# A four-layer graph attention kernel on one core: one pool for the forms of the rows and of elu, an 18th weight buffer, one copy of G further ahead, and other due groups

## The chip, the core and the metric

The kernel runs on one core of one Trainium2 chip. The metric is the device time of one execution in microseconds (us); the time of the kernel before is the median of three runs. Engines are named as the profile names them: PE (TensorE's matmuls), PEld (its loads of stationary operands), DVE (VectorE), ACT (ScalarE), POOL (GpSimd) and SP (SyncE, which issues nearly all DMAs here).

## What is computed

Sixteen graphs of 1024 nodes with 256 features share one adjacency matrix and pass through four graph attention layers, each behind a normalisation and with a residual. Layers 0 and 2 have four heads of 64, layers 1 and 3 one head of 256. The reference, cut to layers 1 and 3 (in layers 0 and 2 the same is done for each head):

```python
# for l in 0..3
h = jnp.maximum(_layernorm(x, axis=-1), 0.0)
x = x + gat_l(h, adj, W_l, a_l)

# layer 1
Wh = jnp.matmul(h, W)
e_src = jnp.matmul(Wh, a[:D]); e_dst = jnp.matmul(Wh, a[D:])
e = e_src + jnp.swapaxes(e_dst, 1, 2)
e = jnp.where(e > 0, e, ALPHA * e)          # leaky ReLU, 0.2 (0.01 in layer 3)
e = jnp.where((adj > 0)[None], e, -jnp.inf)
h_prime = jnp.matmul(jax.nn.softmax(e, axis=-1), Wh)
return jax.nn.elu(h_prime)                  # relu in layer 3
```

## The kernel before

*Tiles and steps.* A graph is held as 8 blocks of 128 nodes. The work is 64 steps, each one layer of one graph; four graphs are in flight, and `order_of_steps` interleaves them so that from step 7 on a four-head step (odd numbers, to 59) and a one-head step (even numbers) alternate. A pair of steps takes 74.6 us. n is the number of a step below.

*A step on TensorE.* The exponential of a leaky ReLU is written as a product of factors of row and column and a maximum: W[j, i] = max(G[i], r[j]) * mask[j, i]. `broadcast` (L383) copies the row G of a head, spread over 128 partitions, from an SBUF buffer gs into PSUM; `weights` (L388) makes a tile W of 128 x 1024 on VectorE, eight per head; `aggregate` (L404) multiplies W with the projected rows `whx` and adds up in PSUM, and ScalarE takes the result out (L419). A step has eight groups k of such matmuls: in a four-head step a head and half of its nodes, in a one-head step one block. Some 3.5 to 3.7 us of matmuls make a group. PSUM has four `bank` buffers for the results and two for G.

*Preparing a step.* `preparation(n)` returns 21 pieces in a fixed order: statistics of each half of the rows (L240, VectorE), their combination (POOL), normalisation of each half (L285, ACT), then for each half its transposition and four projections (L327 on PE, taken out by ACT at L329), and then `factors`, `rows`, the fetch of G's rows and a mark. A half is transposed by DMA: `split` (L294, ACT) separates the two 16-bit halves of each value, a DMA on SP (L296) transposes them, and `merge` (L302, ACT) puts them together. `rows` transposes the factors on TensorE (L351), copies them (gT, L353) and writes them to DRAM by a DMA on SP (`grow`, L355); `fetch` reads one head's G back, spread over all partitions, by another (`gs`, L371, 512 KB). The piece for the last use of gs is the copy of G (L383) on ACT.

*What sets the order.* Every engine runs its instructions in the order in which they are written, and so does SP, which holds back a DMA until what it needs has arrived, with all behind it. The order comes from a plan. Each kind of step has a tuple of 21 due groups, counted from 8 (n - 2), the start of the step two before: FOUR and SHORT (L50, L51) for four-head steps, ONE and TIGHT for one-head steps, SOON, FIRST and LATE for the beginning and special cases. Index 11 is the split of the second half, index 12 its merge, 7 to 10 and 13 to 16 the projections. In the main loop (L608 to L628), each group does in turn: what is left of its own W tiles, its matmuls (`aggregate`), parts of finishing the step before (`ending`), copies of G ahead (`emit_heads`), a piece of setting up a layer (`later`), the pieces of preparation that are due (`prepare`), and W tiles ahead (`emit_tiles`), up to 6 or 3 beyond those made, and no more than WBUFS beyond those used up. `fetch_heads` issues the fetches of gs up to two heads ahead of the copies of G.

*Finishing a step.* `finish` divides by the sum, applies elu and adds to x. elu has a buffer `e` of 128 x 1024 for each half (L447); its parts are due at groups 0 to 3 of the next step, results of layer 3 are stored at group 4.

*Buffers.* The pool `prep` has two buffers `e` and five `rows` (HBUFS), used for all forms of the rows (normalised, split, transposed, merged); `work` has 17 buffers for W (WBUFS). Each of them is 4 KB per partition. A pool hands out the buffer that was released longest ago, and the first instruction on it waits for its last reader.

*Setting up a layer.* `weight_columns(l)` makes columns of the weights from the attention vectors in four pieces: `vectors` (a DMA into a buffer `e`, L141), `spread` (a matmul and a copy on ACT, L149 and L152), `columns` (VectorE, L159 and on) and `bound`. For layers 1 to 3 they are done in the main loop, at groups 0, 1, 2 and 8 from 1, 27 and 43 (L605 to L607).

Of the kernel before, what the change touches and what calls it, by code (L numbers as in the profile page):

```python
# [26 lines left out]
F32 = mybir.dt.float32  # L27
# [9 lines left out]
P = 128  # L37
EPS = 1e-5
SHIFT = 60.0
STREAMS = 4  # L40
WBUFS = 17
HBUFS = 5

# [1 line left out]

FOUR = (-8, -8, -5, 0, 2, 1, 4, 5, 5, 5, 5, 3, 4.5, 5, 5, 5, 5, 6, 8, 8, 10)  # L50
SHORT = (-4, -4, -4, 0, 2, 1, 4, 5, 5, 5, 5, 3, 4.5, 5, 5, 5, 5, 6, 8, 8, 10)  # L51
ONE = (2, 2, 2, 3, 4, 3, 5, 7, 7, 7, 7, 4, 7, 8, 8, 8, 8, 8, 11, 11, 12)
SOON = (0, 0, 0, 1, 2, 1, 3, 4, 4, 5, 5, 2, 5, 6, 6, 7, 7, 7, 8, 8, 10)
FIRST = (-4, -4, -4, -2, -0.9, -1, -1, -0.8, -0.8, -0.8, -0.8, 0, 0, 1, 1, 1, 1, 1, 2, 2, 4)
# [13 lines left out]
def kernel(ctx: ExitStack, tc: tile.TileContext, x, adj, ws, avs, out):  # L68
# [64 lines left out]
    def weight_columns(l):  # L133

        H, slope, hs, _ = LAYERS[l]
        D = F // H
        st = {}

        def vectors(queue=nc.sync):

            st["a"] = prep.tile([P, HALF, H, D], F32, name="e")  # L141
            queue.dma_start(
                out=st["a"][0:1, 2:4],
                in_=bass.AP(tensor=avs[l].tensor, offset=avs[l].offset,
                            ap=[[0, 1], [D, 2], [hs, H], [1, D]]))

        def spread():
            pa = bank(2, H, D)
            nc.tensor.matmul(pa.rearrange("p t h d -> p (t h d)"), lhsT=ones[0:1, :],  # L149
                             rhs=st["a"][0:1, 2:4].rearrange("p t h d -> p (t h d)"),  # L150
                             start=True, stop=True)
            nc.scalar.activation(st["a"][:, 0:2], pa, AF.Copy)  # L152

        def columns(ks=range(K)):
            for k in ks:
                for part in range(2):
                    prod = st["a"][:, 2 + part]
                    wk = heads_of(wx[l], H)[:, k]
                    nc.vector.tensor_mul(prod, wk[:, :, 0:D], st["a"][:, part])  # L159
                    nc.vector.tensor_reduce(  # L160
                        wk[:, :, D] if part else wx[l][:, k, F + H:F + 2 * H], prod, AX.X, ALU.add)
            if K - 1 not in ks:
                return
            st["sq"] = small.tile([P, K, H], F32, name="sq", bufs=1)
            wd = heads_of(wx[l], H)[:, :, :, D]
            nc.vector.tensor_tensor(st["sq"], wd, wd, op=ALU.mult)

        def bound():

            pn = bank(H)  # L170
            for k in range(K):
                nc.tensor.matmul(pn, lhsT=ones, rhs=st["sq"][:, k, :], start=(k == 0),
                                 stop=(k == K - 1))
            top = small.tile([P, 1], F32, name="top", bufs=1)
            nc.vector.tensor_reduce(top, pn, AX.X, ALU.max)
            nc.gpsimd.tensor_tensor(top, top, half1, op=ALU.pow)
            nc.gpsimd.tensor_scalar(cbias[l], top, 16.01, None, op0=ALU.mult)
            nc.gpsimd.tensor_scalar(nbias[l], top, -16.01 * slope, None, op0=ALU.mult)
            nc.gpsimd.tensor_scalar(rbias[l], top, -16.01 * (1.0 - slope), SHIFT,
                                    op0=ALU.mult, op1=ALU.add)  # L180

        return vectors, spread, columns, bound
# [242 lines left out]
    def finish(n):  # L425

        b, l = steps[n]
        H = LAYERS[l][0]
        D = F // H
        st = state[n]  # L430

        def views(half):
            s = slice(half * HALF, (half + 1) * HALF)
            return (xs[b][:, s, :].rearrange("p c (h d) -> p (c h) d", h=H),
                    st["y"][:, s, :, 0:D].rearrange("p c h d -> p (c h) d"),
                    st["r"][:, s, :].rearrange("p c h -> p (c h)"))

        def divide():
            st["r"] = small.tile([P, C, H], F32, name="r")
            nc.vector.reciprocal(st["r"], st["y"][:, :, :, D])  # L440

        def scaled(half):
            xh, yh, r = views(half)
            rb = r[:, :, None].to_broadcast([P, HALF * H, D])
            if l < L - 1:

                e = st["e", half] = prep.tile([P, HALF * H, D], F32, name="e")  # L447
                if H > 1 and slack(n):
                    nc.vector.scalar_tensor_tensor(e, yh, 0.0, rb, op0=ALU.min, op1=ALU.mult)  # L449
            nc.gpsimd.tensor_tensor(yh, yh, rb, op=ALU.mult)  # L450
            if l < L - 1 and not (H > 1 and slack(n)):
                nc.gpsimd.tensor_scalar(e, yh, 0.0, -3.0e38, op0=ALU.min, op1=ALU.max)  # L452

        def exponential(half):
            if l < L - 1:
                nc.scalar.activation(st["e", half], st["e", half], AF.Exp)  # L456

        def add(half):
            xh, yh, r = views(half)
            if l < L - 1:  # L460
                e = st["e", half]
                nc.vector.scalar_tensor_tensor(e, e, -1.0, yh, op0=ALU.add, op1=ALU.max)  # L462
                nc.gpsimd.tensor_add(xh, xh, e)  # L463
                return
            nc.vector.scalar_tensor_tensor(xh, yh, 0.0, xh, op0=ALU.max, op1=ALU.add)  # L465

        def store(half):
            nc.sync.dma_start(
                out=out[b].rearrange("(p c) f -> p c f", p=P)[:, half * HALF:(half + 1) * HALF],
                in_=xs[b][:, half * HALF:(half + 1) * HALF, :])  # L470
            if half == 1 and b + STREAMS < B:
                load(b + STREAMS)


        at = (0, 0, 0, 0, 1, 1, 1) if slack(n) and H > 1 else (0, 0, 1, 1, 2, 2, 3)
        return list(zip(at, (divide, lambda: scaled(0), lambda: scaled(1), lambda: exponential(0),
                             lambda: exponential(1), lambda: add(0), lambda: add(1)))) + (
                    [(4, lambda: store(0)), (4, lambda: store(1))] if l == L - 1 else [])
# [38 lines left out]
    def emit_heads(i):  # L517

        while done["g"] <= min(i + C // 2, done["tiles"] + C, len(tiles) - 1):
            n, h, _ = tiles[done["g"]]  # L520
            if n >= done["prepared"]:
                break
            broadcast(n, h)
            done["g"] += C
            fetch_heads()
# [13 lines left out]
    for n, (b, l) in enumerate(steps):  # L539

        free = -99
        if b % STREAMS in last:
            over = last[b % STREAMS] + 1
            free = 8 * over + (8 if l == 0 else 2 if LAYERS[steps[over][1]][0] == 1 else 4)
        last[b % STREAMS] = n
        start = 8 * (n - 2)
        kind = ONE if LAYERS[l][0] == 1 else SOON if n < 5 else FOUR
        if kind is FOUR and free > start + kind[0]:
            kind = SHORT
        if kind is ONE and free > start + kind[0]:  # L550
            kind = TIGHT
        if free > start + kind[0]:
            kind = LATE
            start = max(free, agenda_of[-1][0] + 5, start - LATE[7])
        agenda_of.append([start + k for k in kind] if n > 1 else FIRST)
        if n > 2:

            assert agenda_of[n][7] >= 8 * (n - 2)
            assert agenda_of[n][3] >= agenda_of[n - 1][12]
    ending = []  # L560
    later = {}
    with tc.manual_schedule():
# [40 lines left out]
            load_weights(i)  # L603

        for l, at in ((1, 1), (2, 8 * 3 + 3), (3, 8 * 5 + 3)):  # L605
            for i, piece in zip((0, 1, 2, 8), layer[l]):
                later[at + i] = piece  # L607
        for n in range(len(steps)):  # L608
            for k, (h, i0, per) in enumerate(groups(n)):
                while planned < len(steps) and min(  # L610
                        a[0] for a in agenda_of[planned:planned + 2]) <= 8 * n + k:
                    plan(planned)
                    planned += 1
                emit_tiles(place[n, h, C - 1] + 1, must=True)
                aggregate(n, h, i0, per)
                if i0 + per == C:
                    done["free"] = place[n, h, C - 1] + 1
                while ending and ending[0][0] <= k:
                    ending.pop(0)[1]()
                upto = min(done["tiles"] + (6 if per > 1 else 3), done["free"] + WBUFS)  # L620
                emit_heads(upto - 1)
                if 8 * n + k in later:
                    later[8 * n + k]()
                prepare(8 * n + k)
                emit_tiles(upto)
            for _, piece in ending:
                piece()
            ending = finish(n) if n < len(steps) - 1 else []  # L628
# [35 lines left out]
```

## Time and profile before

| | |
|---|---|
| median of 3 runs | 2482.13 us (2480.15 to 2482.95) |
| profiled execution | 2481.52 us |
| its span | 2479.7 us |
| mean granted TensorE clock | 0.992 |
| instructions of L404 on PE | 36864, 1909.4 us busy |
| instructions of L327 on PE | 2048, 487.3 us busy |
| W tiles (L388, DVE) | 1280, 1540.8 us busy, 1274 ns each |
| copies of y (L419, ACT) | 504, 191.9 us busy |
| transposes by DMA (L296) | 124 |
| fetches of G (L371) | 159, 512 KB each |

The span is the time between the first and the last instruction of the profiled execution; the rest of its time lies around it. A line of a group names the code's line, engine, operation, and the buffers written and read; busy time is the sum over its instructions. Busy matmuls are modelled at their ends. A number in square brackets on a line of the timeline is how long the engine was idle before it, with what ended that. SP's lines show the issue of a DMA, not its transfer: when a transfer lands is read from the trace's marks of landing.

### The profile page before, as it was taken

The page shows a single profiled execution, that of the slowest core. Times are in us where ns is not written, and L with a number is a line of the kernel's source. Part 1 is how long each engine was busy: PE and PEld are TensorE (multiplying, and loading weights), DVE is VectorE, ACT ScalarE, POOL GpSimd, SP SyncE. Part 2 cuts the span into 40 slices and gives each one's busy share as a digit, 9 for nine tenths or more (in the row PEclk, how much of TensorE's full clock was granted, in tenths as well). Part 3 has the DMA queues.
Part 4 walks back from the last instruction along what each step waited for, and adds up shares of the span by engine and source line. Part 5 has one row for each costly group of instructions (what it writes and reads, how often), then busy time and mean ns, then how long its engine had stood idle before and what let it go on. Part 6 is the DMA issues. An engine that isn't in the chain of part 4 may idle for free.

```text
span 2479.7 us, 86492 instructions
## 1 busy us (share of the span) xinstructions
PE 2403.9 (97%) x39104; PEld 2158.6 (87%) x39104; DVE 2044.1 (82%) x2138; ACT 1482.8 (60%) x2501; POOL 1071.2 (43%) x1366
## 2 busy tenths in 40 slices
PE   7899999999999999999999999999999999999989
PEld 5788898898898888888889888889888898888878
DVE  8997677888888988888888888888888888887963
ACT  5465666556665556755556765656655566666451
POOL 3235455443344444544433554543444444554341
PEclk9999999999999999999999999999999999999999
DMA  4322232333433322323433322223334322323221
GB/s 179 80 54 61 44 79 53 78 96 79 112 72 93 79 55 52 79 62 103 109 91 88 79 62 70 70 55 94 95 76 106 104 55 61 79 56 75 72 52 60
DMA packets 294760, 193.39 MB, mean 78 GB/s; under 512 B 264182, under 2 KB 266998, under 8 KB 292472
## 3 DMA queue, kind: packets, MB, share of 16 engines
q1 hardware_dynamic: 294382, 187.86, 30.5%
q8 instruction: 306, 5.01, 0.8%
q14 instruction: 62, 0.51, 0.1%
q10 hardware_dynamic: 10, 0.00, 0.0%
HBM read 105.39 MB, written 17.43 MB: 50 GB/s over the span
## 4 chain that ended last, share of the span: by engine, by line
PE 86%; DVE 6%; DMA 3%; ACT 3%; issue 2%; POOL 1%; DVEq 0%; SPq 0%; ACTq 0%; POOLq 0%
PE bank L404 68%; PE bank L327 17%; DVE w L388 4%; DMA rows<-rows 3%; ACT rows L302 1%; DVE bn L240 1%; ACT rows L285 0%; DVE e L462 0%; ACT rows L294 0%; POOL rstd L273 0%; DVE mask L213 0%; POOL x L463 0%; DMA x<-in_x 0%; PE bank L351 0%; DVE wx L160 0%
## 5 line engine op out<-in xcount | busy, mean ns | idle before, releaser
L404 PE MATMUL bank<-whx,w 128*64 128x65 f32 x36864 | 1909.4, 241 | 40.1 <-DVE w L388 27.5
L404 PEld LDWEIGHTS bank<-whx,w 128*64 128x64 f32 x36864 | 1755.3, 145 | 200.6 <-DVE w L388 33.8
L388 DVE SCALAR_TENSOR_TENSOR w<-g,rcol,mask 128x1024 f32<-128x1024 f32 x1280 | 1540.8, 1274 | 232.6 <-PE bank L404 135.9
L339 POOL TENSOR_TENSOR whx<-whx 128x1024 f32<-128x1024 f32 x128 | 243.4, 1902 | 858.8 <-ACT whx L337 858.8
L419 ACT ACTIVATE y<-bank 128x260 f32<-128x260 f32 (+1 forms) x504 | 191.9, 384 | 658.1 <-PE bank L404 657.8
L327 PE MATMUL bank<-wx,rows 128*128 128x264 f32 (+1 forms) x2048 | 487.3, 392 | 14.5 <-ACT rows L302 7.5
L327 PEld LDWEIGHTS bank<-wx,rows 128*128 128x128 f32 x2048 | 383.6, 192 | 89.4 <-ACT rows L302 15.5
L450 POOL TENSOR_TENSOR y<-y,r 128x1024 f32<-128x1024 f32 x126 | 260.7, 2078 | 233.8 <-DVE e L449 180.5
L463 POOL TENSOR_TENSOR x<-x,e 128x1024 f32<-128x1024 f32 x96 | 227.1, 2365 | 179.8 <-DVE e L462 179.8
L285 ACT ACTIVATE rows<-x,shift,rstd 128x256 f32<-128x256 f32 x512 | 264.6, 589 | 65.6 <-POOL shift L279 64.0
L329 ACT ACTIVATE whx<-bank 128x264 f32<-128x264 f32 (+1 forms) x512 | 189.4, 385 | 170.3 <-PE bank L327 169.9
L302 ACT ACTIVATE rows<-rows 128x2048 uint16<-128x2048 uint16 x124 | 265.7, 2143 | 21.1 <-DMA rows<-rows 21.1
L294 ACT ACTIVATE rows<-rows 128x2048 uint16<-128x2048 uint16 x124 | 236.2, 1905 | 2.2
L462 DVE SCALAR_TENSOR_TENSOR e<-e,y 128x1024 f32<-128x1024 f32 x96 | 190.9, 1989 | 50.1 <-ACT e L456 41.5
L240 DVE BATCH_NORM_STATS2 bn<-x 128x6 f32<-128x256 f32 x512 | 175.5, 410 | 33.2 <-POOL x L463 30.0
L383 ACT ACTIVATE g<-gs 128x1024 f32<-128x1024 f32 x159 | 162.7, 1023 | 27.1 <-DVE w L388 15.1
L273 POOL TENSOR_TENSOR rstd<-rstd,neghalf 128x4 f32<-128x4 f32 (+1 forms) x97 | 120.2, 1239 | 15.0 <-DVE shift L274 7.6
L456 ACT ACTIVATE e<-e 128x1024 f32<-128x1024 f32 x96 | 100.8, 1050 | 1.0 <-POOL e L452 1.0
L440 DVE RECIPROCAL r<-y 128x32 f32<-128x32 f32 (+1 forms) x63 | 17.3, 275 | 82.9 <-ACT y L419 82.8
L449 DVE SCALAR_TENSOR_TENSOR e<-y,r 128x1024 f32<-128x1024 f32 x58 | 68.5, 1222 | 2.1
L465 DVE SCALAR_TENSOR_TENSOR x<-y,x 128x1024 f32<-128x1024 f32 x30 | 36.5, 1218 | 8.9 <-POOL y L450 8.9
L337 ACT ACTIVATE whx<-whx,nbias 128x16 f32<-128x16 f32 (+1 forms) x128 | 40.3, 315 | 4.2
(67 smaller groups left out, 443.6 us busy)
## 6 DMA issues: line engine op xcount, KB each, us to landing
gs<-grow SPq DMA_DIRECT2D x159, 512.0 KB
x<-in_x SPq DMA_DIRECT2D x15, 1024.0 KB
out<-x SPq DMA_DIRECT2D x30, 512.0 KB
w<-in_adj SPq DMA_DIRECT2D x8, 512.0 KB
rows<-rows SPq DMA_TRANSPOSE x124
x<-in_x SPq DMA_DIRECT2D x2, 512.0 KB
wx<-in_L_gnn_W SPq DMA_DIRECT2D x8, 128.0 KB
out<-x SPq DMA_DIRECT2D x8, 128.0 KB
```

Source lines behind the costliest of these rows:

```text
L240: nc.vector.bn_stats(bn[:, c, :], xs[b][:, c, :])
L285: nc.scalar.activation(xn[:, :, q, :], xs[b][:, c, :].rearrange("p (k i) -> p k i", k=K), AF.Relu, bias=st["shift"][:, c:c + 1], scale=st[ ...
L294: nc.scalar.activation(bits, xn.rearrange("p (n s) -> p s n", s=2), AF.Copy)
L302: nc.scalar.activation(st["hT", half].rearrange("p k i -> p (k i)").bitcast(U16).rearrange("p (n s) -> p n s", s=2), st["turned", half].re ...
L327: nc.tensor.matmul(pw, lhsT=st["hT", half][:, k, q * P:(q + 1) * P], rhs=wx[l][:, k, :], start=(k == 0), stop=(k == K - 1))
L339: nc.gpsimd.tensor_tensor(wh[:, :, :, 0:D], wh[:, :, :, 0:D], wh[:, :, :, D:D + 1].to_broadcast([P, HALF, H, D]), op=ALU.mult)
L388: nc.vector.scalar_tensor_tensor(w, state[n]["g", h], state[n]["rcol"][:, jc, h:h + 1], masks[LAYERS[steps[n][1]][3]][:, jc, :], op0=ALU.m ...
L404: nc.tensor.matmul(acc[o % P:o % P + cols, q, :], lhsT=st["w", h, jc][:, o:o + cols], rhs=st["whx"][:, jc, h * (D + 1):(h + 1) * (D + 1)], ...
L419: nc.scalar.activation(st["y"][:, i0:i0 + per, h, :], acc, AF.Copy)
L450: nc.gpsimd.tensor_tensor(yh, yh, rb, op=ALU.mult)
L462: nc.vector.scalar_tensor_tensor(e, e, -1.0, yh, op0=ALU.add, op1=ALU.max)
L463: nc.gpsimd.tensor_add(xh, xh, e)
```

## The change

- WBUFS goes from 17 to 18, HBUFS from 5 to 6. The buffers `e` of elu come from the pool of `rows`; the buffer for a layer's attention vectors comes from that of W.
- Index 11, the split of a second half, is due at group 2 instead of 3 in FOUR and SHORT.
- A new tuple NEXT takes the place of SHORT where the step two before is not followed by a one-head step. This holds for n = 60 alone, the last four-head step, which follows another four-head step; all its pieces but the first three are due two to four groups later.
- `emit_heads` in the last two groups of a one-head step looks 4 tiles further ahead, which brings the copy of the third head's G of the next step from that step's first group to group 6 of the one-head step.
- For layers 1 to 3, `columns` follows directly behind `spread` in one group.

```diff
-WBUFS = 17
-HBUFS = 5
+WBUFS = 18
+HBUFS = 6
-FOUR = (-8, -8, -5, 0, 2, 1, 4, 5, 5, 5, 5, 3, 4.5, 5, 5, 5, 5, 6, 8, 8, 10)
-SHORT = (-4, -4, -4, 0, 2, 1, 4, 5, 5, 5, 5, 3, 4.5, 5, 5, 5, 5, 6, 8, 8, 10)
+FOUR = (-8, -8, -5, 0, 2, 1, 4, 5, 5, 5, 5, 2, 4.5, 5, 5, 5, 5, 6, 8, 8, 10)
+SHORT = (-4, -4, -4, 0, 2, 1, 4, 5, 5, 5, 5, 2, 4.5, 5, 5, 5, 5, 6, 8, 8, 10)
+NEXT = (-4, -4, -4, 2, 4, 3, 6, 9, 9, 9, 9, 4, 8, 9, 9, 9, 9, 10, 11, 11, 13)
...
-            st["a"] = prep.tile([P, HALF, H, D], F32, name="e")
+            st["a"] = work.tile([P, HALF, H, D], F32, name="w", bufs=WBUFS)
...
-                e = st["e", half] = prep.tile([P, HALF * H, D], F32, name="e")
+                e = st["e", half] = prep.tile([P, HALF * H, D], F32, name="rows",
+                                                    bufs=HBUFS)
...
         if kind is FOUR and free > start + kind[0]:
-            kind = SHORT
+            kind = SHORT if slack(n - 2) else NEXT
...
         for l, at in ((1, 1), (2, 8 * 3 + 3), (3, 8 * 5 + 3)):
-            for i, piece in zip((0, 1, 2, 8), layer[l]):
-                later[at + i] = piece
+            vectors, spread, columns, bound = layer[l]
+            later[at] = vectors
+            later[at + 1] = lambda spread=spread, columns=columns: (spread(), columns())
+            later[at + 8] = bound
...
                 upto = min(done["tiles"] + (6 if per > 1 else 3), done["free"] + WBUFS)
-                emit_heads(upto - 1)
+                emit_heads(upto - 1 + (C // 2 if per == 1 and k >= C - 2 else 0))
```

## The prediction

> **What bounds the kernel now.** I read the page first (busy shares, then the chain that ended last), then busy time by window, then the waits of TensorE in the steady stretch, and last the timelines of ScalarE, SyncE and TensorE around those waits. From the page:
>
> ```profile
> PE 2403.9 (97%) x39104; PEld 2158.6 (87%) x39104; DVE 2044.1 (82%) x2138; ACT 1482.8 (60%) x2501; POOL 1071.2 (43%) x1366
> ...
> PE 86%; DVE 6%; DMA 3%; ACT 3%; issue 2%; POOL 1%; DVEq 0%; SPq 0%; ACTq 0%; POOLq 0%
> ```
>
> TensorE is busy 2403.9 of 2479.7 us, and the change leaves its instructions alone, so all there is to move is 75.8 us of idle time. By window (columns: window, length, then busy time of PE, PEld, DVE, ACT and POOL):
>
> ```profile
> 320.00:2270.00 1950.00, 1925.22 (x31686) 1734.05 (x31685) 1644.19 (x1672) 1214.90 (x2042) 879.22 (x1112) 1.00 0.32 79
> ```
>
> So the steady 1950 us idle 24.8; the row before it, the ramp from 40 to 320 us, has 260.50 busy of 280 and idles 19.5. What TensorE waits for in the steady stretch (waiting group, releaser, then total us, number of waits and the longest):
>
> ```profile
> PE bank L404 <- issue: 11.2, 10, 1.9
> PE bank L327 <- ACT whx L329: 5.9, 8, 1.3
> PE bank L404 <- DVE w L388: 5.7, 26, 0.2
> ```
>
> Once per pair of steps (74.6 us) there is 0.22 us for a tile of W, and then a longer gap, under "issue" or under L329. The pair at 1486 us, ScalarE, SyncE (start, us issuing) and TensorE:
>
> ```profile
> 1483.57 2.07 ACT L285 ACTIVATE rows<-x,shift,rstd 128x256 f32<-128x256 f32 x4
> ...
> 1486.28 1.89 ACT L294 ACTIVATE rows<-rows 128x2048 uint16<-128x2048 uint16 x1
> ...
> 1492.69 1.02 ACT L383 ACTIVATE g<-gs 128x1024 f32<-128x1024 f32 x1
> 1495.97 0.39 ACT L419 ACTIVATE y<-bank 128x260 f32<-128x260 f32 x1 [2.26 <-PE bank L404]
> 1496.26 2.13 ACT L302 ACTIVATE rows<-rows 128x2048 uint16<-128x2048 uint16 x1
> 1498.30 0.93 ACT L329 ACTIVATE whx<-bank 128x264 f32<-128x264 f32 x3
> ```
> ```profile
> 1482.48 2.18 SPq L296 DMA_TRANSPOSE rows<-rows  x1
> 1486.40 0.29 SPq L355 DMA_DIRECT2D grow<-gT  x1
> 1487.89 0.33 SPq L371 DMA_DIRECT2D gs<-grow  x1
> 1488.28 3.60 SPq L296 DMA_TRANSPOSE rows<-rows  x1
> ```
> ```profile
> 1487.18 6.86 PE L404 MATMUL bank<-whx,w 128*64 128x65 f32 x226 [0.22 <-DVE w L388]
> 1495.61 0.33 PE L404 MATMUL bank<-whx,w 128*64 128x65 f32 x2 [1.56 <-issue]
> 1495.87 7.39 PE L327 MATMUL bank<-wx,rows 128*128 128x264 f32 x32
> ```
>
> The reader is to see a chain: normalise, split (L294), last transpose (call it T4; T3 is the one at 1482.48), merge (L302), first eviction of a projection (L329), and TensorE's fifth projection. The fifth needs the second half's rows and a bank that L329 empties behind that merge. I define its due time: the factors' transpose on TensorE (1485.72 here) plus 0.20, plus 256 matmuls of 29.8 ns, plus four projections of 0.887, in all 11.38 us later. Here it is due at 1497.10 and starts at 1499.53, a loss of 2.43. Done so for the 24 pairs from 436 us to 2234 us, the loss is 1.25 us on average in the 11 pairs beside an L3 step (0.55 to 2.12), and 1.59 in the 13 beside an L1 step (0.77 to 2.77). These include the 0.22 and the "issue" gaps.
>
> **What the Trainium skill says.** "DMA: Bandwidth & Descriptors", section "Queues, rings and completion order": a DMA's semaphore is a strongly ordered write, which lands only after every earlier write from that DMA engine. The trace agrees. A grow that is issued with no transpose in flight lands 1.2 us later (1338.12 to 1339.34), and one that is issued behind a flying transpose lands just after it (1486.40 to 1487.88, T3 landing at 1487.70; 1411.91 to 1413.27, T3 at 1413.10; 157.22 to 160.16, the transpose at 160.16). "TensorE: Matmul & The Clock Gate", section "What's actually happening": an idle window of about 3.4 us drops the clock. In the trace a gap of 3.46 us at 257.64 is followed by 228 matmuls in 8.44 us, where 6.87 is usual; gaps near 2 us are followed by the usual rate.
>
> **The change, part by part.**
>
> *Split of the second half, index 11 of FOUR and SHORT, 3 to 2.* It is met 27 times. On SyncE the order T3, grow, gs, T4 becomes T3, T4, grow, gs; on ScalarE the split comes directly behind normalise and ahead of the eviction of group 3 and of gT. T4 itself goes earlier: here normalise ends at 1485.64, so split ends and T4 is issued at 1487.54 instead of 1488.28. But grow is now behind a flying transpose, and gs waits on SyncE for grow's landing, with G (L383), the eviction of y and the merge queued behind gs on ScalarE. From T4's issue: landing 4.3 (transposes alone take 4.25 to 4.3), grow 0.17 behind it, gs 3.5 (alone 3.3 to 3.7), wake and G 1.1, eviction 0.3: the merge starts 9.4 us after T4, then 2.1 for it and 0.4 for the first L329. Here: 1487.54 + 9.4 + 2.5 = 1499.44, a loss of 2.34 against 2.43. The same sum for each pair gives 2.33 on average beside L1 (13 x (2.33 - 1.59) = +9.7 us) and 1.15 beside L3 (11 x (1.15 - 1.25) = -1.1). Beside L3, the results are stored from 1343.3 on in the pair at 1338, and gs would be issued at 1342.6 and share the DMA engines with them. The trace has no gs beside stores alone; bounds are 0 and 2.3 us (the longest gs landing, 5.8 beside T4, less 3.5). I take 0.5: 11 x 0.5 = +5.5. Three occurrences before 436 us, where other waits cover: +1 (0 to +3). Steady sum +15.
>
> *WBUFS 17 to 18, and HBUFS 5 to 6 with e moved into the pool.* The sum of the 4 KB buffers is the same (17 + 5 + 2, then 18 + 6). One W tile more ahead of the add of elu removes the 0.22 us wait, but the fifth projection then waits 0.22 longer: it is already in the loss above, so 0. T4's target is the buffer released longest ago, which is T3's source, so T4 also waits for T3's landing (T3 + 4.3): earlier than the split's end (T3 + 4.8 to 5.1), cost 0. The e's first merge waits for the add of the elu, finished some 2 us before: 0; without that cover up to 2 us in each of the 13 pairs.
>
> *One copy of G further ahead.* The third head's G goes from the first group of the four-head step to group 6 of the one-head step before. ScalarE is 62% busy there (1214.9 of 1950): 1 us moved, cost 0 (bounds 0 and 0.4 x 24, if an eviction behind it is late). VectorE gets no gap removed that TensorE waits on, except in the ramp.
>
> *Columns of layer 1 directly behind the spread.* VectorE is the bound in the early ramp, and TensorE's longest gap there waits for it (timeline, VectorE's row and TensorE's):
>
> ```profile
> 48.34 20.34 DVE L388 SCALAR_TENSOR_TENSOR w<-g,rcol,mask 128x1024 f32<-128x1024 f32 x17
> ...
> 257.64 8.44 PE L404 MATMUL bank<-whx,w 128*64 128x65 f32 x228 [3.46 <-DVE w L388]
> ```
>
> It now reaches the columns at about 62.7 and must wait for the copy (L152, ends 65.14): +2.4, which with the statistics behind it makes some +3.2. Against it, in the step before 257 us two W tiles now come ahead of bn_stats: gaps of 2.37 and 3.46 and the slow matmuls after (8.44 - 6.87 = 1.6) are 7.4, of which I take 5.6 since the tiles are not all in time. Ramp: -2.4 (bounds +3.2 and -6).
>
> *NEXT.* It holds for n=60 alone: eight projections (7.3 us of TensorE) move from beside n=58 to n=59. A VectorE wait of 7.35 us at 2288.8 goes, and the chain of statistics to the last projections starts about 3.3 us earlier: -3.3 (bounds 0 and -8).
>
> Sum: +15 - 2.4 - 3.3 = +9 on the profiled execution's 2481.5 (span 2479.7), and the median of the runs is 0.6 above it: 2491 us.
>
> **Rivals.** (A, not slower) grow is not held by T4: with a landing 1.2 us after its issue, gs lands about 3 us earlier than I sum, the merge waits only for T4, and the losses at the fifth projection go almost to 0.3: 24 x 1.1 = -26, less the ramp and the end, 2450 at best; with a partial hold 2470. Place: the landing of grow. Price: each 0.1 us earlier is 2.4 us in all. It decides from 0.4 us on (9 / 24). For it: grow is 4 KB; against it the three landings above. (B, no change) The chain is as I sum, but the ramp and the end give their full bounds, or gs beside stores costs nothing: 2480 to 2486. For it: L3 pairs come out even. (C, much slower) the "issue" gaps, most of which end 0.2 to 0.5 us after a landing of gs or T4 (1495.61 here, T4 landing at 1495.42), come again with the later gs and add 0.5 to 1.2 us in each pair: +12 to +29, 2503 to 2520. Against it: T4 and gs no longer fly together. (D) The change does not do what it says: the order of instructions on SyncE does change, so only the sizes are open.
>
> **How the numbers follow.** Forecast 0.46 (2486 to 2497), A 0.17, B 0.18, C 0.19. A measurement of this kernel tells about 0.2% from no change, 5 us. Faster: A and a little of B, 0.19. Within: most of B, some of the forecast's lower edge, 0.18. Slower 0.63. The range leaves out A's far end and C's far end: 2468 to 2512.
>
> **What would show it.** The forecast is right if after the change gs is issued some 4.5 us after T4, and G, the eviction and the merge follow it without pause, with L327 waiting on L329 in nearly all pairs and 1 us longer beside L1 than beside L3. The 0.22 waits on W should be gone. A is right if gs is issued under 2 us after grow. The ramp is right if the gap at 257 is gone. It would be wrong, too, if the 18th buffer let VectorE run far enough ahead to move something else, such as the adds of elu, onto the path of the statistics.

## The result and the profile after

| | before | after |
|---|---|---|
| median | 2481.14 us (2479.22 to 2482.95, 4 runs) | 2543.82 us (2537.19 to 2554.20, 4 runs) |
| profiled span | 2479.7 us | 2541.2 us |

The ratio is 1.0257 (95% interval 1.0221 to 1.0292): slower, which was forecast, but by 63 us and not by 9, and above the range given (2468 to 2512).

The page of the kernel after: busy shares, the chain that ended last, and the two groups of TensorE (busy us, mean ns, then idle us before them and what ended most of it). The lines of the code stand one or two lower than before.

```profile
PE 2427.0 (96%) x39104; PEld 2163.2 (85%) x39104; DVE 2045.6 (80%) x2138; ACT 1478.4 (58%) x2501; POOL 1075.5 (42%) x1366
...
PE 77%; DMA 8%; ACT 7%; DVE 5%; issue 2%; POOL 1%; SPq 1%; DVEq 0%; ACTq 0%; POOLq 0%
...
L405 PE MATMUL bank<-whx,w 128*64 128x65 f32 x36864 | 1905.6, 241 | 27.6 <-DVE w L389 15.5
...
L328 PE MATMUL bank<-wx,rows 128*128 128x264 f32 (+1 forms) x2048 | 512.9, 403 | 63.7 <-ACT y L420 28.0
```

The chain shows a new owner: DMA 8% and ACT 7%, 3% each before. The time is in one group. Idle time ahead of the projections is 63.7 us where it was 14.5 (+49.2), the projections themselves are busy for 512.9 us where it was 487.3 (+25.6), and the W matmuls give back 12.5 us of idle time and 3.8 of busy time. The sum is +58.5 of the 61.5 us by which the span grew. The second figure had not been foreseen. Some 15 us of it are matmuls at a lower clock (below). Most of the rest is how busy time is counted: a row of 32 matmuls without a wait shows 7.39 us, the same 32 in three parts at the full rate 2.94 + 1.16 + 3.83 = 7.93 us.

The waits of TensorE from 320 to 2330 us (total us, number, longest):

```profile
PE bank L328 <- ACT y L420: 28.0, 21, 2.9
PE bank L328 <- ACT whx L330: 27.9, 26, 1.2
PE bank L405 <- issue: 5.1, 8, 0.9
PE bank L328 <- ACT rows L303: 2.1, 3, 1.2
```

The 0.22 us waits on W are gone, as forecast, and the "issue" gaps have fallen from 11.2 us to 5.1. In all 26 pairs of steps a projection waits for the first L330, and in 21 the one before it waits for an eviction of y. The pair at 1440 us, ScalarE, SyncE and TensorE in the timeline:

```profile
1438.61 2.07 ACT L286 ACTIVATE rows<-x,shift,rstd 128x256 f32<-128x256 f32 x4
1440.71 1.91 ACT L295 ACTIVATE rows<-rows 128x2048 uint16<-128x2048 uint16 x1
1442.53 0.37 ACT L420 ACTIVATE y<-bank 128x260 f32<-128x260 f32 x1
1442.80 0.25 ACT L354 ACTIVATE gT<-bank 8x128 f32<-8x128 f32 x1
...
1451.49 1.03 ACT L384 ACTIVATE g<-gs 128x1024 f32<-128x1024 f32 x1 [4.09 <-DMA gs<-grow]
1452.46 0.37 ACT L420 ACTIVATE y<-bank 128x260 f32<-128x260 f32 x1
1452.72 2.13 ACT L303 ACTIVATE rows<-rows 128x2048 uint16<-128x2048 uint16 x1
```
```profile
1437.52 8.51 SPq L297 DMA_TRANSPOSE rows<-rows  x2
1446.09 0.47 SPq L356 DMA_DIRECT2D grow<-gT  x1
1448.06 0.34 SPq L372 DMA_DIRECT2D gs<-grow  x1
```
```profile
1448.59 2.94 PE L328 MATMUL bank<-wx,rows 128*128 128x264 f32 x12
1452.88 1.16 PE L328 MATMUL bank<-wx,rows 128*128 128x264 f32 x4 [1.36 <-ACT y L420]
1455.19 6.84 PE L328 MATMUL bank<-wx,rows 128*128 128x264 f32 x16 [1.16 <-ACT whx L330]
```

gT is ready at 1443.05, but SyncE has just begun to issue T4 (1443.07) and issues grow only at 1446.09. The trace's landing marks have T4 at 1447.86 and grow at 1448.05; gs is issued at 1448.06 and lands at 1451.47. ScalarE stands idle for 4.09 us for it, although the transposed rows have been there for 3.6, because the merge is queued behind G and an eviction. And the sixteen matmuls of the last four projections take 6.84 us instead of 3.83. The next view shows why. Its windows give the length, busy PE, PEld, DVE, ACT and POOL, then the granted clock of TensorE; two are of this pair and two of the pair at 363 us. They are cut where the trace's clock records can change: these stand on a grid of 3.41 us, and each grants the full clock or half of it.

```profile
1451.09:1454.50 3.41, 1.59 (x6) 0.69 (x5) 2.54 (x3) 3.00 (x3) 0.00 (x0) 1.00 0.00 0
1454.50:1461.33 6.83, 6.14 (x14) 4.80 (x15) 6.83 (x7) 3.30 (x10) 1.90 (x1) 0.50 0.00 0
...
372.48:375.89 3.41, 1.87 (x9) 1.26 (x7) 2.02 (x2) 0.98 (x2) 0.00 (x0) 1.00 0.41 144
375.89:379.30 3.41, 1.86 (x7) 1.31 (x8) 3.33 (x3) 3.41 (x7) 0.00 (x0) 1.00 0.00 0
```

The waits of 1.36 and 1.16 us, with only four matmuls between them, leave TensorE 1.59 us of work in one window of the grid, and the next 6.83 us run at half the clock. The pair at 363 us waits longer, 1.95 and 1.15 us, but the grid parts its waits: 1.87 and 1.86 us of work, and the clock stays. So it is throughout: from 340 to 2320 us of the changed kernel nine stretches at half the clock begin, each behind a window with at most 1.59 us of work, and none begins behind a window with 1.68 us or more. Which pairs are hit depends on where their waits fall on the grid, and not on their length alone.

With the prediction's measure (the factors' transpose on TensorE plus 11.38 us is when the fifth projection is due; the loss counts to the last projection) the 26 pairs from 360 to 2290 us lose, on average:

| | beside L1 (14) | beside L3 (12) | 26 pairs |
|---|---|---|---|
| before | 1.74 us | 1.32 us | 40 us |
| after | 4.33 us | 2.97 us | 96 us |

So 56 of the 61.5 us are in this one place. (The first expectation below has 3.95 and 51 us, because slow ends of a few projections are missing from its figures.) The prediction's own figures for the kernel before, 1.59 and 1.25 us at the fifth projection in 24 pairs with 2.77 the longest, come out of the trace as 1.65 and 1.29 in the 25 pairs of that stretch, with 4.33 in the pair at 436 us. That lowers its steady sum by 1 us and changes nothing else.

### The profile page after: what moved, and what is told of

It is laid out like the page before. It is cut to its first block, busy times and chain, and to the rows that moved or that the text cites. A ratio compares the mean times of both kernels' runs of the same rounds, so it can differ in the third digit from the quotient of the medians.

```text
span 2541.2 us, 86579 instructions
## 1 busy us (share of the span) xinstructions
PE 2427.0 (96%) x39104; PEld 2163.2 (85%) x39104; DVE 2045.6 (80%) x2138; ACT 1478.4 (58%) x2501; POOL 1075.5 (42%) x1366
## 4 chain that ended last, share of the span: by engine, by line
PE 77%; DMA 8%; ACT 7%; DVE 5%; issue 2%; POOL 1%; SPq 1%; DVEq 0%; ACTq 0%; POOLq 0%
PE bank L405 61%; PE bank L328 16%; DMA gs<-grow 4%; DVE w L389 3%; DMA grow<-gT 3%; ACT rows L303 2%; ACT rows L286 1%; ACT rows L295 1%; ACT y L420 1%; SPq L297 1%; ACT g L384 1%; DVE bn L241 0%; DVE rows L464 0%; DMA rows<-rows 0%; ACT whx L330 0%
## 5 line engine op out<-in xcount | busy, mean ns | idle before, releaser
L328 PE MATMUL bank<-wx,rows 128*128 128x264 f32 (+1 forms) x2048 | 512.9, 403 | 63.7 <-ACT y L420 28.0
L328 PEld LDWEIGHTS bank<-wx,rows 128*128 128x128 f32 x2048 | 390.5, 197 | 158.0 <-ACT whx L330 39.4
L465 POOL TENSOR_TENSOR x<-x,rows 128x1024 f32<-128x1024 f32 x96 | 227.1, 2366 | 180.0 <-DVE rows L464 180.0
L330 ACT ACTIVATE whx<-bank 128x264 f32<-128x264 f32 (+1 forms) x512 | 188.7, 388 | 180.2 <-PE bank L328 179.9
L464 DVE SCALAR_TENSOR_TENSOR rows<-rows,y 128x1024 f32<-128x1024 f32 x96 | 192.6, 2006 | 43.6 <-ACT rows L458 36.3
L458 ACT ACTIVATE rows<-rows 128x1024 f32<-128x1024 f32 x96 | 100.7, 1049 | 0.2 <-POOL rows L454 0.2
L451 DVE SCALAR_TENSOR_TENSOR rows<-y,r 128x1024 f32<-128x1024 f32 x58 | 70.2, 1251 | 2.5 <-DVE r L441 0.5
```

The lines of the kernel that those rows point to most:

```text
L328: nc.tensor.matmul(pw, lhsT=st["hT", half][:, k, q * P:(q + 1) * P], rhs=wx[l][:, k, :], start=(k == 0), stop=(k == K - 1))
L330: nc.scalar.activation(st["whx"][:, c, :], pw, AF.Copy)
```

## The experiments

Each run is compared with the kernel before on the same chip; what is given is the ratio to it, with its interval.

**The split of the second half alone, taken out (e1) and put in (e2).**

```diff
# e1, on the changed kernel (SHORT alike); e2 is the reverse, on the kernel before
-FOUR = (-8, -8, -5, 0, 2, 1, 4, 5, 5, 5, 5, 2, 4.5, 5, 5, 5, 5, 6, 8, 8, 10)
+FOUR = (-8, -8, -5, 0, 2, 1, 4, 5, 5, 5, 5, 3, 4.5, 5, 5, 5, 5, 6, 8, 8, 10)
```

> The changed kernel with the split of the second half due at group 3 again (FOUR and SHORT); pools, G ahead, NEXT and columns stay as changed. Theory S (order on SyncE: T4 ahead of grow and gs puts the flight of T4 into the chain grow, gs, G, merge, fifth projection): the loss before the fifth projection falls from 3.95 (L1) and 2.97 (L3) back to about 1.7 and 1.3 us per pair, the 51 us over 26 pairs come back, time 2478 to 2492. Rival P (the shared pool of six buffers delays the transposes): it stays above 2520. Rival G (the copy of G moved ahead, or the 18th W buffer, moves work on ScalarE or VectorE in the way): it stays above 2520.

> The kernel before with only the split of the second half due at group 2 instead of 3. Theory S: nearly the whole loss, 2525 to 2545, with gs issued about 5.2 us after T4. Rivals P and G: within 10 us of before, 2475 to 2492. If both S and the pools are needed together (T4's target is T3's source only with six buffers): in between, about 2500.

e1: 2486.16 us, ratio 1.0015 (1.0006 to 1.0025), loss 42 us. e2: 2530.26 us, ratio 1.0180 (1.0165 to 1.0196), loss 90 us, gs issued 5.1 us after T4. One index in two tuples is worth 45 us when it is put in alone (0.018 of 2484), and with it taken out 4 us are left. The pools and the copy of G fall as causes of the loss. 45 and 4 us leave 14 of the 63, which appear only where both are together; 6 of them are in the loss (90 against 96 us), and the rest was not traced further.

**ScalarE's order against SyncE's (e3).** The split's ScalarE half stays at group 2, its DMA is a piece of its own, due at group 3, behind grow and gs (at its old place in the other tuples).

```diff
             nc.scalar.activation(bits, xn.rearrange("p (n s) -> p s n", s=2), AF.Copy)
+            if half == 0:
+                turn(half)
+
+        def turn(half):
...
             st["turned", half] = prep.tile([P, 2, K * HALF, P], U16, name="rows", bufs=HBUFS)
             nc.sync.dma_start_transpose(
...
-        out += [factors, rows, lambda: fetch_heads(n + 1), lambda: None]
+        out += [factors, rows, lambda: fetch_heads(n + 1), lambda: turn(1), lambda: None]
```

> The changed kernel with the ScalarE half of the split still at group 2, but its DMA transpose issued at group 3, behind grow and gs as before the change. Theory S (SyncE's order does it, ScalarE's order is harmless): the loss per pair goes to 1.0 to 1.8 us, time 2475 to 2492. Rival A (ScalarE's order does it: the split ahead of the eviction of group 3 and of gT delays grow): it stays near 2530 or falls by less than 15 us.

2506.58 us, ratio 1.0088 (1.0071 to 1.0106): neither. The loss is 60 us, 1.49 per pair beside L3, nearly as before, but 2.98 beside L1. There gT comes behind the split, so grow and gs are later, and T4 behind them on SyncE is issued 7.3 us after T3 instead of 6.0. ScalarE's order costs too, if the transpose stays behind gs: theory S had called it harmless and was wrong in that.

**Whether grow is held by T4, or stands behind it (e4).**

```diff
-            nc.sync.dma_start(out=st["grow"].rearrange("h c i -> c h i"), in_=gT)
+            nc.scalar.dma_start(out=st["grow"].rearrange("h c i -> c h i"), in_=gT)
```

> The changed kernel with grow issued from ScalarE's queue directly behind gT, so that it no longer stands behind T4's issue on SyncE (T4 + 2.1 us), gs still on SyncE. Theory S with the hold (grow's semaphore lands only behind the transposes already in flight, whichever queue): gs is still issued 4.4 to 5.2 us after T4, time within 15 us of the changed kernel, 2525 to 2545. Rival I (only the place in SyncE's queue costs, the landing is not held): grow lands about 1.2 us after gT, gs is issued at about T4 + 3 or as soon as SyncE has issued T4, and the time falls by over 25 us, below 2515.

2488.05 us, ratio 1.0013 (1.0004 to 1.0022): the hold as expected here is refuted. The timeline of e4, SyncE and ScalarE:

```profile
1486.17 6.98 SPq L297 DMA_TRANSPOSE rows<-rows  x2
1493.69 0.61 SPq L372 DMA_DIRECT2D gs<-grow  x1
```
```profile
1491.45 0.25 ACT L354 ACTIVATE gT<-bank 8x128 f32<-8x128 f32 x1
1491.73 0.28 ACTq L356 DMA_DIRECT2D grow<-gT  x1
...
1498.50 1.03 ACT L384 ACTIVATE g<-gs 128x1024 f32<-128x1024 f32 x1 [2.44 <-DMA gs<-grow]
```

T4 was issued at 1491.30 and landed at 1497.39. grow, issued 0.43 us after it from the other queue, landed by 1493.67, well before it, and gs followed at once. In all 26 pairs of e4 grow lands ahead of T4, by 0.7 to 5.4 us; in 22 of them it was issued behind it. In the changed kernel, on one queue, it lands level with T4 or up to 0.6 us behind in 18, 1.3 to 1.5 us behind in 3 and 1.4 us ahead in 5. So the hold is one within a queue, and not a strict one. The trace's record of DMA packets agrees: in this pair T4's packets run from 1.18 to 4.02 us after its issue, and grow's eight packets run among them, at 1.63 to 1.91. In the changed kernel grow's packets start at 3.56 or later in all 26 pairs, as those of T4 come to their end. On average gs is issued 5.2 us after T4 in the changed kernel and 2.5 in e4. Of these 2.7 us, 1.9 are grow's issue (2.1 us after T4 against 0.3) and 1.0 its landing (3.0 us after its issue against 2.0); in e4 gs then waits 0.3 us more on average, where SyncE is still issuing T4.

**What the merge's place behind G costs (e5, e6).** e5 is the changed kernel with index 12 of FOUR and SHORT at 4 instead of 4.5; e6 has e4's edit as well.

```diff
-FOUR = (-8, -8, -5, 0, 2, 1, 4, 5, 5, 5, 5, 2, 4.5, 5, 5, 5, 5, 6, 8, 8, 10)
+FOUR = (-8, -8, -5, 0, 2, 1, 4, 5, 5, 5, 5, 2, 4, 5, 5, 5, 5, 6, 8, 8, 10)
```

> The changed kernel with the merge of the second half due at group 4 instead of 4.5 (FOUR and SHORT), so that on ScalarE it stands before the copy of G and the eviction of y. Theory Q (the chain T4, grow, gs, G, eviction, merge, first L330 carries the loss, because the merge is queued behind G although T4 landed 5 us earlier): the merge leaves the end of the chain, the fifth projection starts about 1.8 us earlier in each of 26 pairs, loss about 2.1 (L1) and 1.2 (L3), time 2490 to 2505. Rival L (the late landing of T4 itself holds the fifth projection): no change, within 8 us of 2543.

> The changed kernel with both: grow issued from ScalarE's queue, and the merge of the second half ahead of G. Theory Q: G starts about 7.5 us after T4, the fifth projection is free at T4 + 9.4, in time in pairs beside L3 and 0.3 us late beside L1; the loss of 47 us in all goes to 5 to 15, time 2448 to 2468, below both kernels. Rival F (TensorE's pauses under issue are what is left and do not depend on this chain): no lower than 2480.

e5: 2499.14 us, ratio 1.0083 (1.0058 to 1.0108), loss 59 us. e6: 2467.19 us, ratio 0.9944 (0.9924 to 0.9963), loss 18 us, faster than both kernels. The waits of TensorE from 320 to 2270 us, of e5 and of e6:

```profile
PE bank L328 <- ACT y L420: 31.9, 21, 3.2
PE bank L405 <- issue: 4.7, 8, 0.9
PE bank L328 <- ACT rows L303: 1.5, 3, 1.0
```
```profile
PE bank L405 <- issue: 5.3, 7, 1.2
PE bank L328 <- ACT y L420: 4.7, 7, 1.4
PE bank L328 <- ACT rows L303: 1.5, 2, 1.2
```

In e5 the wait on the first L330 has gone, and what is left is the fourth projection, which waits for a bank: the eviction of y behind a late G. With grow on its own queue G is mostly in time, and that wait falls from 31.9 to 4.7 us. The time of e6 lies at the upper end of what was expected; its loss is 18 us where 5 to 15 were foreseen.

**Controls on the kernel before (e7, e8).** e7 is the kernel before with e4's edit alone; e8 has the split at 2, the merge at 4 and grow on ScalarE's queue, without the rest of the change.

> The kernel before with only grow moved to ScalarE's queue. Theory I (what grow pays is its place behind T4 on SyncE's queue): in the kernel before grow stands ahead of T4 and mostly behind a landed T3, so there is little to gain, 2474 to 2484. If the queue of grow is worth something by itself, the time falls by over 15 us.

> The kernel before with three edits: the split of the second half at group 2, its merge at 4, grow on ScalarE's queue; pools, copies of G, NEXT and columns as before. Theory Q: the same gain as in the changed kernel with these edits, less 0.2 us per pair for the late W tile: 2450 to 2475. Rival P (without the shared pool and the 18th buffer the early split has no use): 2480 or more.

e7: 2477.24 us, ratio 0.9985 (0.9977 to 0.9993), loss 33 us. With T4 behind grow there is little to gain. e8: 2469.80 us, ratio 0.9959 (0.9946 to 0.9973), loss 26 us. Its interval overlaps that of e6: the early split pays without the shared pool, the 18th buffer, the copy of G further ahead and NEXT.

**The small terms (e9 to e12).** (The expectations count the steps from 1 here; the text counts them from 0 throughout.) e9 is e6 with SHORT in place of NEXT; e10 is e6 with the columns in a group of their own again; e11 is the kernel before with only the buffers changed; e12 joins e9 and e10.

```diff
# e9
-            kind = SHORT if slack(n - 2) else NEXT
+            kind = SHORT
# e10
-            vectors, spread, columns, bound = layer[l]
-            later[at] = vectors
-            later[at + 1] = lambda spread=spread, columns=columns: (spread(), columns())
-            later[at + 8] = bound
+            for i, piece in zip((0, 1, 2, 8), layer[l]):
+                later[at + i] = piece
```

> The fastest kernel so far (the changed one with grow on ScalarE's queue and the merge of the second half at group 4, 2467 us) with SHORT in place of NEXT for n = 60. If the prediction's term for NEXT is right (-3.3 us), this kernel is 3 us slower, 2470. If NEXT only moves the wait (in the run with the split at group 3 the delay against before was 1.9 us at n = 58 and 2.3 at the end), the time is the same within 2 us.

> The same kernel with the columns of layers 1 to 3 in a group of their own behind the spread, as before the change. The prediction's ramp term has +3.2 us for VectorE's wait at the spread. In the trace of the fastest kernel the delay against before rises by 4.9 us at n = 2 and falls by 3.9 at n = 6. If the columns are its cause and the W tiles of n = 4 its cure: 3 to 5 us faster, 2462 to 2464. If both belong to the same edit: the same within 2 us.

> The kernel before with only the buffers changed (WBUFS 18, HBUFS 6, elu's e in the pool of rows, the attention vectors in that of W). The prediction costs this at nothing in the steady stretch: 2476 to 2486, with the 0.22 us waits on W gone and the fifth projection waiting as long in their place. Rival P (the shared pool delays transposes): 2490 or more.

> Grow on ScalarE's queue, the merge of the second half at group 4, the columns in a group of their own and SHORT in place of NEXT, all else as changed. From the traces: the columns cost 5.1 us at n = 2 and NEXT 2 us at the end. If both are so, 2455 to 2459; if NEXT is worth nothing either way, 2458 to 2461.

e9: 2464.75 us, ratio 0.9935 (0.9921 to 0.9950), not to be told from e6. e10: 2458.73 us, ratio 0.9909 (0.9895 to 0.9923), the fastest here and below the 2462 expected at the least. e12: 2460.10 us, ratio 0.9913 (0.9900 to 0.9926), not to be told from e10, as expected if NEXT is worth nothing either way. The columns cost some 6 us: e9 and e10, on the same chip, differ by 6.0, but in NEXT as well; e9 and e12 differ in the columns alone, and their ratios, taken on two chips, are 5.5 us apart. In e10's trace the rise of the delay at n = 1 is gone, while the fall of 3.8 us at n = 5 stays.

e11: 2476.72 us, ratio 0.9984 (0.9975 to 0.9993), some 4 us less. Its waits from 320 to 2270 us:

```profile
PE bank L327 <- ACT whx L329: 16.2, 14, 2.7
PE bank L404 <- issue: 11.4, 8, 2.3
```

The 5.7 us for W have left the list, and the wait on L329 has grown from 5.9 to 16.2 us. That is what the prediction said: what the 18th buffer gives at one end of the chain is taken at the other, as long as the merge ends it. But this profile is of the slowest of e11's 22 runs (2483.89 us), so it shows where the waits go and not what they cost.

## Why the prediction was wrong

*The bound and the place: right.* The change lost its time where the prediction looked, at the fifth projection behind the merge, and the direction was right. The 0.22 us waits on W vanished; with the buffers they were worth some 4 us where the prediction had 0 (e11). The copy of G was not run alone; what is left in e1, 4 us, is no more than the columns cost.

*The step that failed: the sum for the steady stretch, "the merge starts 9.4 us after T4", +15 us in all.* It measured +56. Two terms failed: the landing of T4 at 4.3 us, with the links that hang on it, and the clock after a wait, put at nothing.

First, the chain itself. The fifth projection was forecast at 13.71 us after the factors' transpose beside L1 and 13.03 beside L3; it came at 14.71 and 14.06, on average 1.0 us later in 26 pairs, some 26 us. The parts: T4 was issued 5.30 us after T3 beside L1 instead of 5.06 (it waited for T3's landing, costed at 0); gs was issued 5.2 us after T4 instead of 4.5, because T4 landed after 5.1 to 5.2 us and not after 4.3; gs took 3.7 beside L1 instead of 3.5, and 4.4 beside L3 instead of 4.0. From gs's landing to the fifth projection the sum was right within 0.2 us. "Transposes alone take 4.25 to 4.3" holds for some half of the transposes in the trace before that have no large transfer beside them, but not for those in this place: T3, also without one, took 4.29 to 6.05 us there, 5.04 on average (the prediction itself shows one of 5.22, 1482.48 to 1487.70). The same misreading put T4's wait for T3's landing at 0. The chain had no slack left to hide it.

Second, the clock. The prediction read that gaps near 2 us are followed by the usual rate. That was wrong, and the trace of before had one against it: the gap of 1.94 us that ends at 445.37. On the grid of the clock records it is

```profile
442.20:445.62 3.42, 1.48 (x51) 1.34 (x47) 3.42 (x4) 1.61 (x2) 0.24 (x1) 1.00 1.29 121
445.62:449.03 3.41, 3.41 (x43) 2.98 (x38) 3.41 (x4) 1.91 (x3) 0.00 (x0) 0.50 0.20 47
```

TensorE worked for 1.48 us in one window, the next has half the clock, and 32 matmuls of the projections take 8.11 us instead of 7.39. A window empty of work was not needed. The change made such waits longer, and many of them are two waits with a short burst between, so that more windows fall below 1.6 us of work. The sixteen matmuls from the fifth projection on take 3.44 us from first to last start at full clock; in 9 of the 26 pairs they took 4.1 to 6.5, on average 4.34 beside L1 and 3.63 beside L3, together 15 us. With the 26 us of the chain that is the 41 us that the sum missed. The prediction followed only the fifth projection; the fourth, which waits for a bank behind G and the eviction of y, does not delay the fifth in the sum, but splits the pause in two.

*Ramp and end, forecast -2.4 and -3.3: about nothing.* In e1, where the steady stretch is as before, the kernel is 0.7 us behind the kernel before at the start of n = 5, 1.9 at n = 57 and 2.3 at the end. The columns cost 5.1 us by the start of n = 1 (forecast 3.2). By that of n = 5 they are made up, 3.8 of them in n = 4, where W tiles now come ahead of the statistics (forecast 5.6): the gaps of 2.37 and 3.46 us have become four of 0.85, but the 228 matmuls behind them still take 8.44 us. NEXT took the wait of 7.35 us away; VectorE waits 8.46 us for a copy of G instead, at 2325 us, and the end is not earlier.

*The Trainium skill's sentence on strongly ordered writes.* "DMA: Bandwidth & Descriptors", section "Queues, rings and completion order", has the semaphore land behind earlier writes of that DMA engine across its queues. The prediction used it for any transpose in flight. On one queue the runs agree with a hold; across two queues, e4 shows none for a transpose that was issued 0.43 us earlier and is still flying, with packets before and after those of grow. Rival A, a grow that is not held, was therefore wrong for the changed kernel and right in its mechanism for e4. The price given for it, 2.4 us in all for each 0.1 us, would have given 65 us for the 2.7 us by which gs came earlier in e4; e4 gained 56.

*Rival C* had the size (2503 to 2520 at most, still too low) by another mechanism: the "issue" gaps did not grow with the later gs, they fell to 5.1 us.

## What to carry to other kernels

Moving a transfer ahead in a queue moves all behind it back: write down the chain that hangs on the one which is overtaken, to its end on the busiest engine, before pricing the one which is moved. If two transfers of one queue feed one engine in order, look first for a second queue and for a consumer that can be taken in the order in which the data lands; here those two edits turned a loss of 2.6% into a gain of 0.6%, and of 0.9% with the columns as before. Price a chain without slack at the mean and the range that its links have in that very place of the trace, not at the shortest found elsewhere, and ask what the clock does after the wait.

## What the runs showed of the hardware

- A 4 KB write that was issued from another queue behind a DMA transpose in flight landed after 2.1 us on average, ahead of the transpose in 22 of 22 pairs (e4). Issued from the same queue, it landed level with the transpose or behind it in 21 of 26 (the changed kernel).
- In the traces before and after, the granted clock of TensorE is full or half, and between 340 and 2320 us half the clock lasts 3.41 us or twice that. In the changed kernel it begins there behind windows with at most 1.59 us of work on TensorE, and behind none with 1.68 or more; over all fourteen traces of this case in that stretch the border lies between 1.4 and 1.7 us of 3.41. A wait far shorter than a window is enough, if it falls within one: 1.94 us at 445 us before, 1.36 and 1.16 us at 1455 us after. Two waits that the grid parted left the clock full (1.95 and 1.15 us, from 374 us on).
- The flight of T4 falls in two groups, 4.2 to 4.8 us (13 of 26 pairs in the changed kernel) and 5.7 to 6.0 (10). In 8 of the 10 slow ones its packets end as early as in the others, 3.8 to 4.0 us after the issue; only the landing comes late. It goes with fetches of instructions, which the trace lists as packets of 16 KB and less in queues of their own. Of the transposes with no large transfer beside them, those with no such packet from 1.2 to 4.2 us after their issue landed after 4.23 to 4.40 us (53 before, 50 after the change), and those with one after 4.23 to 6.05, on average 5.0 (37) and 4.9 (63). No run moved the fetches, so that they are the cause is not shown.
